# GATv2 on one Trainium2 core: order of the gathers, the table products and the logits in a three-layer edge loop

## The chip, the core and the metric

The kernel runs on one core of a Trainium2 chip. A core has five engines that work side by side, each through its own instructions in order: TensorE (PE in the profile, with its weight loads as PEld), VectorE (DVE), ScalarE (ACT), GpSimd (POOL) and SyncE (SP, which here only starts transfers). They meet through semaphores. The matmul's results go to PSUM, which is cut into eight banks of 128 x 512 float32. Transfers between the device's memory and SBUF are started by SP, ACT and POOL.

The metric is the time of one execution in microseconds. The kernel before takes 4618.6 us, the median of three runs (4614.17 to 4620.98).

## What is computed

The whole program is a four-layer network on 1250 nodes with 512 features; the change lies in its first stage, a GATv2 of three layers. Cut to what matters:

```python
src2 = concatenate([src, loop]); dst2 = concatenate([dst, loop])
ea2 = concatenate([edge_attr, mean_ea])
for k in range(3):
    xl = x @ Wl[k] + bl[k]
    xr = x @ Wr[k] + br[k]
    ef = ea2 @ We[k]
    m = leaky_relu(xl[src2] + xr[dst2] + ef, 0.2)
    logit = m @ att[k]
    alpha = segment_softmax(logit, dst2)
    out = segment_sum(xl[src2] * alpha[:, None], dst2) + b_out[k]
    h = out + x
    x = relu(layernorm(h) * gamma[k] + beta[k])
```

For every edge the row `xl` of its source is fetched, the row `xr` of its destination and the edge's own term are added, and a weighted sum over the features gives the logit. The softmax runs over the edges that end at one node; the weighted sum of the fetched rows is the node's new value.

## The kernel before

The edges are sorted by destination and cut into 12 blocks of 107 nodes. A layer has 188 tiles of 128 edges (`FT`), in 47 groups of four (`FG`, `GE = 4`); four groups make a block. `gat_layer` (L1198) runs one layer; its main loop (L1421 to L1445) takes one tile per step `i`, with `g, j = divmod(i, 4)`, and calls the small functions below; a framework turns their instructions into the engines' queues, with the waits that data and buffers ask for, and may move an instruction some places in its queue.

What one group goes through:

- `load(g)` (L1223): four gathers on POOL (L231), each fetching 128 rows `xl` of 513 numbers from the table `tl` (the 513th is the linear part of the logit), into one of nine buffers; at the head of a block the destinations' rows `hl` (SP, L1231 and L1232); the mask `nb` (SP, L1235, four buffers) and the edges' features, written straight into the one-hot tile `oh` (SP, L1237, three buffers). Called for groups 0 to 2 before the loop, then for g + 3 at j = 1.
- `onehot(g)` (L1243): ACT turns the mask into the one-hot matrix; for g + 1 at j = 2.
- `right(i)` (L1256, L1257): two matmuls on PE multiply the one-hot tile with the destinations' rows, high and low part, into an `mm` bank. For odd tiles under 16 (`on_pe`) a third (L1259) adds `xl`.
- `logits(i)` (L1269, L1272): VectorE adds `xl` to the bank (where PE has not), takes the negative part times `att` and sums it into `lg`. It runs one tile behind `right`.
- `spread(g)` (L1278, L1279, L1283, L1287): two VectorE adds of 128 x 4 bring the linear parts of node and edge into `lg`; PE transposes spread the logits; VectorE masks them and keeps the running minimum. At the end of a block ACT takes the exponentials (L1296), and `turn` (L1312, L1315) and `mix` (L1325, a bank of `more`) of the block's groups are put on the list `edge`, one mix a step. The last mix of a group frees its `xl` buffer.
- `finish(b)` (L1333): VectorE adds the residual `cur`; then a list `todo` of due steps: `norm`, `scale`, `relu` (with the multiplication by gamma and the addition of beta on POOL, L1368 and L1369, and the store), `across` (PE transposes L1378, ACT copies), and in layers 1 and 2 the products of the finished nodes with the next layer's weights, `gat_tables` (L1150): eight matmuls per 128 nodes (L1161; four into one `mm` bank for the left table, four for the right one), each pair of four followed by the eviction on ACT and VectorE (L1169, L1171; L1177, L1178) and a store by SP (L1173, L1179). The next layer's first gather waits for the last of these stores.
- `load_cur(b)` (L1408): SP loads the block's own rows `c`, and POOL adds `b_out` to them (L1413). `prepare` loads the next layer's weights and vectors, all at step 6.

The PSUM banks are `mm` 4, `tp` 2 (transposes), `more` 2. The products take turns with the edge tiles in the four `mm` banks. The list `todo` gives up one entry a step, two when it holds more than twelve. After the loop the rest of `edge` and `todo` is worked off, two of each at a time (L1446).

Of the kernel before, what the change touches and what calls it, by code (L numbers as in the profile page):

```python
# [37 lines left out]
GE = 4  # L38
# [19 lines left out]
class Net:  # L58
# [46 lines left out]
    @contextmanager  # L105
    def psum(self, mm=4, tp=4, more=0):

        with self.tc.tile_pool(name="psum", bufs=1, space=bass.MemoryType.PSUM) as self.ps:
            self.banks = {"mm": mm, "tp": tp, "more": more}
            yield  # L110

    @contextmanager
# [997 lines left out]
    def gat_weights(self, L, p):  # L1110


        nc, I, k = self.nc, self.I, L["k"]
        L["wl"] = self.weight(I["L0_gnn_Wl"][k], 4, D)
        L["wr"] = self.weight(I["L0_gnn_Wr"][k], 4, D)
        v = p.tile([128, D], F32, tag="v", name="we")
        nc.sync.dma_start(v[0:2], I["L0_gnn_We"][k])
        nc.sync.dma_start(v[2:3], I["L0_gnn_bl"][k].unsqueeze(0))
        more = p.tile([128, D], F32, tag="v", name="br")
        nc.gpsimd.memset(more[:16], 0.0)  # L1120
        for i in range(2):
            nc.sync.dma_start(L["tr"][NP:, i, :], more[:16])
        nc.sync.dma_start(L["ends"][:8, 1, :], more[:8])
        nc.sync.dma_start(more[2:3], I["L0_gnn_br"][k].unsqueeze(0))
        nc.gpsimd.tensor_tensor(v[:3], v[:3], more[:3], op=ALU.add)
        hl = p.tile([128, 2, D], F32R, tag="tro", name="wehl")
        nc.scalar.copy(hl[:3, 0], v[:3])
        nc.gpsimd.tensor_tensor(hl[:3, 1], v[:3], hl[:3, 0].bitcast(F32), op=ALU.subtract)
        for r in range(0, 8, 2):
# [17 lines left out]
        nc.vector.scalar_tensor_tensor(L["ae"], self.rec[:, :, 3], cs[1], L["ae"],  # L1147
                                       op0=ALU.mult, op1=ALU.add)

    def gat_tables(self, L, p, t, xT):  # L1150


        nc = self.nc
        ts = slice(t * 128, (t + 1) * 128)
        d = {}

        def product(name, c):
            def f():
                if c == 0:
                    d[name] = self.mm()  # L1160
                nc.tensor.matmul(d[name], lhsT=xT(c), rhs=L[name][:, c, :], start=c == 0,  # L1161
                                 stop=c == 3)
                if c == 3:
                    (left if name == "wl" else right)(d[name])
            return f

        def left(m):
            o = p.tile([128, D + 1], F32, tag="tlo", name="tlo")
            nc.scalar.copy(o[:, :D], m)  # L1169
            junk = p.tile([128, D], F32, tag="junk", name="junk", bufs=1)  # L1170
# [27 lines left out]
    def gat_layer(self, L, p, xtab, otab, big):  # L1198
# [4 lines left out]
        nxt = None if k == 2 else {}  # L1203

        def prepare():
            for name in ("b_out", "bl", "gamma", "beta"):
                vec[name] = p.tile([128, D], F32, tag=name, name=name, bufs=1)
                nc.sync.dma_start(vec[name], I["L0_gnn_" + name][k].unsqueeze(0)
                                  .to_broadcast([128, D]))
            nc.gpsimd.tensor_tensor(vec["b_out"], vec["b_out"], vec["bl"], op=ALU.add)  # L1210
            if nxt is not None:
                nxt.update(self.gat_vectors(k + 1, p))
                self.gat_weights(nxt, p)
                self.gat_linear(nxt, p, p)

        todo = deque()
        edge = deque()
        step = [0]

        def block(g):  # L1220
# [2 lines left out]
        def load(g):  # L1223
# [17 lines left out]
        def onehot(g):  # L1241
            d = G[g]
# [32 lines left out]
        def spread(g):  # L1275
            d = G[g]
            b, k, last = block(g)
            nc.vector.tensor_tensor(d["lg"], d["lg"], d["xl"][:, :, D], op=ALU.add)  # L1278
            nc.vector.tensor_tensor(d["lg"], d["lg"], L["ae"][:, g * GE:(g + 1) * GE],  # L1279
                                    op=ALU.add)  # L1280
# [52 lines left out]
        def finish(b):  # L1333
# [21 lines left out]
            def scale():  # L1355
# [7 lines left out]
                else:  # L1363
                    nc.vector.scalar_tensor_tensor(rs[:R, 1:2], mv[:R, 0:1], -1.0, rs[:R, 0:1],
                                                   op0=ALU.mult, op1=ALU.mult)
                    nc.scalar.activation(h[:R], h[:R], AF.Identity, scale=rs[:R, 0:1],
                                         bias=rs[:R, 1:2])
                    nc.gpsimd.tensor_tensor(h[:R], h[:R], vec["gamma"][:R], op=ALU.mult)  # L1368
                    nc.gpsimd.tensor_tensor(h[:R], h[:R], vec["beta"][:R], op=ALU.add)  # L1369

# [4 lines left out]
            def across():  # L1375
# [30 lines left out]
        cur = {}  # L1406

        def load_cur(b):  # L1408
            R = min(BN, NP - b * BN)
            c = p.tile([128, D], F32, tag="c", name="c")  # L1410
            for lo, hi in ((0, BW),) if b < NB - 1 else ((0, 96), (96, R)):
                nc.sync.dma_start(c[lo:hi], xtab[b * BN + lo:b * BN + hi, :])
            nc.gpsimd.tensor_tensor(c[:R], c[:R], vec["b_out"][:R], op=ALU.add)  # L1413
            cur[b] = c

        for g in range(3):
            load(g)
        onehot(0)  # L1420
        for i in range(FT + 2):  # L1421
            g, j = divmod(i, GE)
            step[0] = i
            if j == 1 and g + 3 < FG:
                load(g + 3)
            if j == 2 and g + 1 < FG:
                onehot(g + 1)
            if i == 6:
                prepare()
            if i % 16 == 8 and i < FT:  # L1430
                load_cur(i // 16)
            if i < FT:
                right(i)
            if 1 <= i <= FT:
                logits(i - 1)
            if j == 1 and 1 <= g <= FG:
                spread(g - 1)
            while edge and edge[0][0] <= i:
                _, f, product = edge.popleft()
                f()  # L1440
                if product:
                    break
            for _ in range(2 if len(todo) > 12 else 1):
                if todo and todo[0][0] <= i:
                    todo.popleft()[1]()  # L1445
        while edge or todo:  # L1446
            for _ in range(2):
                if edge:
                    edge.popleft()[1]()
            for _ in range(2):  # L1450
                if todo:
                    todo.popleft()[1]()
        return nxt

    def run(self, fast):
# [65 lines left out]
    def gat_first(self, pv, xtab):  # L1521
        nc, I = self.nc, self.I
        L = self.gat_vectors(0, pv)
        with self.tc.tile_pool(name="l0", bufs=1) as p, \
# [3 lines left out]
            with self.tc.tile_pool(name="edge", bufs=1, side="right") as pe, \  # L1528
                    self.weights(), self.psum(4, 3, 1):
                self.edge_pool = pe  # L1530
                self.gat_weights(L, pt)
                self.prepare_edges()
                for t in range(NT):
                    self.ready(t)
# [12 lines left out]
                def steps():  # L1547
                    for t in range(NT):
                        for i, f in enumerate(self.gat_tables(
                                L, pt, t, lambda c: xnT[:, c, t * 128:(t + 1) * 128])):  # L1550
                            f()
                            if i % 4 == 3:
                                yield
# [1570 lines left out]
```

## Time and profile before

| | us |
|---|---|
| median of three runs (lowest, highest) | 4618.6 (4614.17, 4620.98) |
| the profiled execution | 4626.03 |
| its span | 4624.2 |
| layer 1 of the stage, first gather to the next layer's first gather | 312.9 to 775.7 |
| layer 2 | 775.7 to 1235.9 |
| layer 3, to its end | 1235.9 to 1661 |
| PE, DVE, ACT, POOL busy over the span | 3950, 2760, 1507, 1361 |
| mean TensorE clock granted | 0.925 of full speed |

The span is the profiled execution from its first to its last instruction. A busy share over the whole span says little, since the program has a dozen stages with different limits; the stage of the change takes 29% of it. Windows (stretches of the span, with each engine's busy time in them) show one stage at a time, and the rows of an engine show what it was doing and, in brackets, how long it had been idle and which instruction released it. "issue" and "remote" there are waits for which the profile names no instruction. A wait is put down to whatever came last.

### The profile page before, as it was taken

What the parts mean: (1) busy time and instruction counts of PE and PEld (TensorE: products, weight loads), DVE (VectorE), ACT (ScalarE), POOL (GpSimd) and SP (SyncE); (2) the same over time, 40 slices, a digit from 0 to 9 for tenths busy, and PEclk for the clock granted to TensorE, in tenths of its full rate; (3) what the DMA queues carried; (4) which work ended last, traced back from release to release, by engine and by line L of the source; (5) the groups of instructions that cost most, each with busy time, mean ns of one, the idle gap of its engine ahead of it and who ended that gap; (6) DMA issues with size and microseconds to landing.
All of it is one profiled execution on the core that took longest, in us unless ns stands there. A gap on an engine that the chain in (4) does not pass through costs nothing.

```text
span 4624.2 us, 49180 instructions
## 1 busy us (share of the span) xinstructions
PE 3950.4 (85%) x15439; PEld 2438.3 (53%) x15454; DVE 2760.3 (60%) x6534; ACT 1506.7 (33%) x2738; POOL 1361.1 (29%) x1198
## 2 busy tenths in 40 slices
PE   6978997899878876799899999997969975898796
PEld 3435553455444443444788877564536553454574
DVE  5358884888488966533796767314693135587301
ACT  2213332343233355111374346222221022455121
POOL 2026663566356501101100000103253003676101
PEclk9998998899989977899999999998989997998798
DMA  6446664566456612411521110382011285565695
GB/s 221 149 124 193 183 190 140 165 185 190 128 168 180 172 63 77 139 33 35 161 65 41 56 34 28 138 318 95 12 54 62 73 271 164 156 202 175 234 339 191
DMA packets 282999, 647.56 MB, mean 140 GB/s; under 512 B 61673, under 2 KB 108905, under 8 KB 267322
## 3 DMA queue, kind: packets, MB, share of 16 engines
q1 hardware_dynamic: 169290, 357.13, 23.7%
q0 software_dynamic: 73088, 234.75, 18.0%
q10 hardware_dynamic: 40352, 52.44, 3.4%
q8 instruction: 126, 2.06, 0.2%
q14 instruction: 143, 1.17, 0.1%
HBM read 528.87 MB, written 120.65 MB: 140 GB/s over the span
## 4 chain that ended last, share of the span: by engine, by line
PE 32%; DVE 9%; DMA 5%; issue 3%; ACT 2%; POOL 1%; SPq 0%; another core or an unknown queue 0%; ACTq 0%; POOLq 0%; DVEq 0%
PE more L2051 5%; PE mm L2601 4%; PE mm L1914 3%; PE mm L179 3%; PE mm L171 3%; PE mm L3039 2%; DMA xe<-routed_in 2%; PE mm L776 2%; PE mm L2295 2%; PE mm L2013 1%; PE more L2877 1%; PE mm L2290 1%; DVE junk L1942 1%; DVE e L1976 1%; PE mm L2405 1%
## 5 line engine op out<-in xcount | busy, mean ns | idle before, releaser
L231 POOL DMA_INDIRECT xl<-xl,srcI x564 | 610.8, 1083 | 404.1 <-PE more L1325 167.6
L1325 PE MATMUL more<-xl,wT 128*128 128x512 f32 x1128 | 584.9, 611 | 5.5 <-ACT wT L1315 5.5
L1256 PE MATMUL mm<-hl,oh 121*128 121x512 f32 x564 | 399.1, 708 | 103.6 <-DVE s L1269 66.7
L1269 DVE TENSOR_TENSOR s<-xl,mm 128x512 f32<-128x512 f32 x540 | 364.0, 680 | 170.2 <-PE mm L1257 80.8
L1272 DVE SCALAR_TENSOR_TENSOR junk<-s,att 128x512 f32<-128x512 f32 x540 | 405.0, 750 | 5.5
L2051 PE MATMUL more<-hh,e 128*128 128x259 f32 x1600 | 384.2, 386 | 11.7 <-ACT o L1994 9.4
L2051 PEld LDWEIGHTS more<-hh,e 128*128 128x128 f32 x1600 | 295.0, 191 | 76.3 <-issue 16.0
L171 PE MATMUL mm<-w,xnT 128*128 128x512 f32 x640 | 307.0, 619 | 13.8 <-DVE xnT L136 5.3
L231 POOL DMA_INDIRECT g<-routed_out,getI x60 | 66.5, 1109 | 681.5 <-DMA routed_out<-o 494.7
L1325 PEld LDWEIGHTS more<-xl,wT 128*128 128x128 f32 x1128 | 207.0, 196 | 92.2 <-issue 44.2
L1257 PE MATMUL mm<-hl,oh 121*128 121x512 f32 x564 | 242.5, 430 | 0.0
L231 POOL DMA_INDIRECT hs<-gcn_h,srcI x188 | 213.5, 1136 | 95.6 <-issue 35.5
L1256 PEld LDWEIGHTS mm<-hl,oh 121*128 121x128 f32 x564 | 112.6, 200 | 226.9 <-issue 115.2
L1243 ACT ACTIVATE oh<-nb 112x512 fp32r<-112x512 bf16 x141 | 88.6, 629 | 356.1 <-DMA nb<-nbt 241.9
L171 PEld LDWEIGHTS mm<-w,xnT 128*128 128x128 f32 x640 | 123.4, 198 | 141.9 <-issue 125.2
L1971 ACT ACTIVATE e<-r,hh 128x512 f32<-128x512 f32 (+1 forms) x240 | 154.1, 646 | 131.8 <-PE more L2051 120.9
L2601 PE MATMUL mm<-form,cw 128*128 128x312 f32 (+1 forms) x640 | 175.5, 436 | 21.8 <-POOL cw L2578 18.2
L2877 PE MATMUL more<-hl,oh 128*128 128x512 f32 x376 | 162.0, 532 | 35.0 <-DVE hl L2838 9.8
L1974 ACT ACTIVATE e<-r,a 128x512 f32<-128x512 f32 (+1 forms) x240 | 152.3, 646 | 70.6 <-DVE e L1976 58.5
L1976 DVE TENSOR_TENSOR e<-e,e 128x512 f32<-128x512 f32 (+1 forms) x240 | 141.6, 596 | 50.9 <-ACT e L1971 44.6
L1315 ACT COPY wT<-tp 128x512 f32<-128x512 f32 x141 | 82.3, 584 | 267.4 <-PE tp L1312 212.8
L160 PE MATMUL tp<-ident,xn 128*128 128x128 f32 x280 | 51.4, 331 | 135.2 <-issue 56.2
(618 smaller groups left out, 7894.0 us busy)
## 6 DMA issues: line engine op xcount, KB each, us to landing
w<-L_ffn_Wp SPq DMA_DIRECT2D x64, 1024.0 KB
w<-L_ffn_table SPq DMA_DIRECT2D x56, 1025.0 KB
neg<-ntab SPq DMA_DIRECT2D x80, 320.0 KB
nb<-nbt SPq DMA_DIRECT2D x141, 128.0 KB
hl<-xr SPq DMA_DIRECT2D x36, 448.0 KB
xr<-tro SPq DMA_DIRECT2D x30, 512.0 KB
xe<-routed_in SPq DMA_DIRECT2D x56, 256.0 KB
routed_out<-o ACTq DMA_DIRECT2D x56, 256.0 KB
```

The source lines that it names most:

```text
L171: self.nc.tensor.matmul(p, lhsT=xT[:, c, t * 128:(t + 1) * 128], rhs=w[:, c, n0:n0 + n], start=c == 0, stop=c == k - 1)
L231: self.nc.gpsimd.indirect_dma_start(out=out, out_offset=None, in_=table, in_offset=bass.IndirectOffsetOnAxis(ap=idx, axis=0), bounds_check ...
L1256: nc.tensor.matmul(m, lhsT=s, rhs=hl[:K, 0, :], start=True, stop=False)
L1257: nc.tensor.matmul(m, lhsT=s, rhs=hl[:K, 1, :], start=False, stop=not on_pe(i))
L1269: nc.vector.tensor_tensor(o, d["xl"][:, j, :D], s, op=ALU.add)
L1272: nc.vector.scalar_tensor_tensor(junk, s, 0.0, L["att"], op0=ALU.max, op1=ALU.mult, accum_out=d["lg"][:, j:j + 1])
L1325: nc.tensor.matmul(B[b]["y"], lhsT=d["wT"][:, j, :], rhs=d["xl"][:, j, :D], start=k == 0 and j == 0, stop=last and j == GE - 1)
L1971: nc.scalar.activation(e1[:, :n], R[q, k, 0][:, :n], AF.Exp, bias=HH[q][:, s, 256:257])
L1976: nc.vector.tensor_tensor(e1[:, :n], e1[:, :n], e2[:, :n], op=ALU.max)
L2051: nc.tensor.matmul(ys[j], lhsT=e[:, j * 128:(j + 1) * 128], rhs=HH[q][:, s, :], start=s == 0, stop=s == NT - 1)
L2601: nc.tensor.matmul(m, lhsT=g[:, which, c, :], rhs=forms[form][:, c, q % 2, q // 2:q // 2 + n], start=j + c == 0, stop=j + 1 == len(gs) and ...
L2877: nc.tensor.matmul(y, lhsT=oh, rhs=hl[:, i], start=i + j == 0 and not (self.fast and k), stop=last and i + j == GE)
```

## The change

What it does, part by part:

- One PSUM bank, `tab`, is set apart for the table products; `mm` has three banks. `gat_tables` is given the function that hands out the bank. The products go to a list of their own, `late`, which gives up one every second step (every step while it holds more than eight); they are put there when `across` is issued. `todo` gives up one a step.
- `load` keeps the gathers and `hl`; the mask and the edge features move to `fields(g)`, called for g + 2 at j = 2 (0 and 1 before the loop).
- `linear(g)`, a POOL add of the two linear parts into `lin` (two buffers), stands at j = 1 ahead of the gathers of g + 3; VectorE's `spread` adds `lin` alone.
- `onehot(g + 1)` moves to j = 1; `logits` runs two tiles behind `right`, `spread` at j = 2; the loop has one step more. `on_pe` covers odd tiles under 20.
- POOL's add on `c` becomes `bias_cur`, twelve steps after the load; gamma and beta become `affine`, five steps after `finish`; `relu` follows at nine and `across` (or the last layer's `add`) at twelve.
- `prepare` and `gat_weights` become generators that go on every third step from step 6.

```diff
-            self.banks = {"mm": mm, "tp": tp, "more": more}
+            self.banks = {"mm": mm, "tp": tp, "more": more, "tab": 8 - mm - tp - more}
...
-    def gat_tables(self, L, p, t, xT):
+    def gat_tables(self, L, p, t, xT, bank):
...
-                    d[name] = self.mm()
+                    d[name] = bank()
...
+            G.setdefault(g, {})["xl"] = xl
+
+        def fields(g):
             nb = p.tile([128, GE * 128], BF16, tag="nb", name="nb", bufs=4)
             nc.sync.dma_start(nb, self.nbt[g])
             s = p.tile([128, GE * 128], F32R, tag="oh", name="oh", bufs=3)
             nc.sync.dma_start(s[BW:K].bitcast(F32),
                               self.eat[:, g * GE * 128:(g + 1) * GE * 128])
-            G[g] = {"xl": xl, "nb": nb, "s": s}
+            G.setdefault(g, {}).update(nb=nb, s=s)
+
+        def linear(g):
+            lin = p.tile([128, GE], F32, tag="lin", name="lin")
+            nc.gpsimd.tensor_tensor(lin, G[g]["xl"][:, :, D], L["ae"][:, g * GE:(g + 1) * GE],
+                                    op=ALU.add)
+            G[g]["lin"] = lin
...
-            return i < 16 and i % 2 == 1
+            return i < 20 and i % 2 == 1
...
-            nc.vector.tensor_tensor(d["lg"], d["lg"], d["xl"][:, :, D], op=ALU.add)
-            nc.vector.tensor_tensor(d["lg"], d["lg"], L["ae"][:, g * GE:(g + 1) * GE],
-                                    op=ALU.add)
+            nc.vector.tensor_tensor(d["lg"], d["lg"], d["lin"], op=ALU.add)
...
+                for t in whole:
+                    for f in self.gat_tables(nxt, p, t, lambda c, t=t: X[t][:, c, :],
+                                             lambda: self.bank("tab", [128, D])):
+                        late.append((step[0] + 1, f))
...
-            todo.extend(((now + 1, norm), (now + 3, scale), (now + 8, relu)))
+            todo.extend(((now + 1, norm), (now + 3, scale), (now + 5, affine),
+                         (now + 9, relu)))
             if nxt is None:
-                todo.extend((now + 11, add(t)) for t in whole)
+                todo.extend((now + 12, add(t)) for t in whole)
             else:
-                todo.append((now + 11, across))
-                for t in whole:
-                    for f in self.gat_tables(nxt, p, t, lambda c, t=t: X[t][:, c, :]):
-                        todo.append((now + 12, f))
+                todo.append((now + 12, across))
...
+        fields(0)
         for g in range(3):
             load(g)
+        fields(1)
         onehot(0)
-        for i in range(FT + 2):
+        prepared = prepare()
+        for i in range(FT + 3):
             g, j = divmod(i, GE)
             step[0] = i
-            if j == 1 and g + 3 < FG:
-                load(g + 3)
-            if j == 2 and g + 1 < FG:
-                onehot(g + 1)
-            if i == 6:
-                prepare()
+            if j == 1:
+                if g < FG:
+                    linear(g)
+                if g + 3 < FG:
+                    load(g + 3)
+                if g + 1 < FG:
+                    onehot(g + 1)
+            if j == 2 and g + 2 < FG:
+                fields(g + 2)
+            if i >= 6 and i % 3 == 0:
+                next(prepared, None)
             if i % 16 == 8 and i < FT:
                 load_cur(i // 16)
+            if i % 16 == 4 and i > 16:
+                bias_cur(i // 16 - 1)
             if i < FT:
                 right(i)
-            if 1 <= i <= FT:
-                logits(i - 1)
-            if j == 1 and 1 <= g <= FG:
+            if 2 <= i < FT + 2:
+                logits(i - 2)
+            if j == 2 and 1 <= g <= FG:
                 spread(g - 1)
...
-            for _ in range(2 if len(todo) > 12 else 1):
-                if todo and todo[0][0] <= i:
-                    todo.popleft()[1]()
-        while edge or todo:
+            if todo and todo[0][0] <= i:
+                todo.popleft()[1]()
+            if late and late[0][0] <= i and (i % 2 == 0 or len(late) > 8):
+                late.popleft()[1]()
+        bias_cur(NB - 1)
+        while edge or todo or late:
...
-        with self.psum(4, 2, 2):
+        with self.psum(3, 2, 2):
             self.gatv2_fast(L, xtab)
```

More of the change, by code (lines that the diff above doesn't have):

```diff
@@ L1124, in gat_weights @@
         nc.sync.dma_start(more[2:3], I["L0_gnn_br"][k].unsqueeze(0))
+        yield
         nc.gpsimd.tensor_tensor(v[:3], v[:3], more[:3], op=ALU.add)
+        yield
         hl = p.tile([128, 2, D], F32R, tag="tro", name="wehl")
         nc.scalar.copy(hl[:3, 0], v[:3])
+        yield
         nc.gpsimd.tensor_tensor(hl[:3, 1], v[:3], hl[:3, 0].bitcast(F32), op=ALU.subtract)
+        yield
         for r in range(0, 8, 2):
@@ L1209, in prepare @@
                                   .to_broadcast([128, D]))
-            nc.gpsimd.tensor_tensor(vec["b_out"], vec["b_out"], vec["bl"], op=ALU.add)
+            steps = iter(())
             if nxt is not None:
                 nxt.update(self.gat_vectors(k + 1, p))
-                self.gat_weights(nxt, p)
+                steps = self.gat_weights(nxt, p)
+                next(steps)
+            yield
+            nc.gpsimd.tensor_tensor(vec["b_out"], vec["b_out"], vec["bl"], op=ALU.add)
+            for _ in steps:
+                yield
+            if nxt is not None:
                 self.gat_linear(nxt, p, p)
@@ L1217, in gat_layer @@
         edge = deque()
+        late = deque()
         step = [0]
@@ L1367, in scale, with affine @@
                                          bias=rs[:R, 1:2])
+            def affine():
+                if not tail:
                     nc.gpsimd.tensor_tensor(h[:R], h[:R], vec["gamma"][:R], op=ALU.mult)
@@ L1412, in load_cur, with bias_cur @@
                 nc.sync.dma_start(c[lo:hi], xtab[b * BN + lo:b * BN + hi, :])
+            cur[b] = c
+        def bias_cur(b):
+            c = cur[b]
+            R = min(BN, NP - b * BN)
             nc.gpsimd.tensor_tensor(c[:R], c[:R], vec["b_out"][:R], op=ALU.add)
-            cur[b] = c
+        fields(0)
         for g in range(3):
             load(g)
+        fields(1)
         onehot(0)
-        for i in range(FT + 2):
+        prepared = prepare()
+        for i in range(FT + 3):
             g, j = divmod(i, GE)
             step[0] = i
-            if j == 1 and g + 3 < FG:
-                load(g + 3)
-            if j == 2 and g + 1 < FG:
-                onehot(g + 1)
-            if i == 6:
-                prepare()
+            if j == 1:
[9 more added lines that the diff above has]
+                next(prepared, None)
             if i % 16 == 8 and i < FT:
                 load_cur(i // 16)
+            if i % 16 == 4 and i > 16:
+                bias_cur(i // 16 - 1)
             if i < FT:
                 right(i)
-            if 1 <= i <= FT:
-                logits(i - 1)
-            if j == 1 and 1 <= g <= FG:
+            if 2 <= i < FT + 2:
+                logits(i - 2)
+            if j == 2 and 1 <= g <= FG:
                 spread(g - 1)
@@ L1452, in gat_layer @@
                     todo.popleft()[1]()
+            for _ in range(2):
+                if late:
+                    late.popleft()[1]()
         return nxt
@@ L1530, in gat_first @@
                 self.edge_pool = pe
-                self.gat_weights(L, pt)
+                for _ in self.gat_weights(L, pt):
+                    pass
                 self.prepare_edges()
@@ L1549, in steps @@
                         for i, f in enumerate(self.gat_tables(
-                                L, pt, t, lambda c: xnT[:, c, t * 128:(t + 1) * 128])):
+                                L, pt, t, lambda c: xnT[:, c, t * 128:(t + 1) * 128],
+                                self.mm)):
                             f()
```

## The prediction

> **What bounds the kernel now.** I read the whole page first, then the windows of the stage that the change touches, then the row of VectorE (DVE) and GpSimd (POOL) at the head of a layer, then the waits. The page's chain of waits reaches back only to 2215 us, so it says nothing here; the stage (three GATv2 layers) lies from 312.9 us, layer 1's first gather, to 1661 us, and what it loses is read from its own windows. Columns: window and length, then busy time (count) of PE, PEld, DVE, ACT, POOL, then clock, DMA share and GB/s.
>
> ```profile
> 776.00:830.00 54.00, 25.67 (x54) 13.40 (x55) 16.76 (x47) 1.05 (x2) 36.24 (x36) 0.56 0.69 195
> 830.00:1180.00 350.00, 324.53 (x1154) 185.66 (x1153) 303.02 (x794) 137.34 (x252) 204.38 (x181) 0.97 0.62 177
> 1186.00:1236.00 50.00, 45.43 (x129) 21.32 (x127) 13.29 (x33) 14.37 (x28) 3.04 (x3) 0.97 0.25 79
> 1236.00:1286.00 50.00, 21.65 (x49) 10.30 (x48) 13.00 (x35) 1.26 (x2) 35.92 (x36) 0.70 0.72 204
> 1286.00:1630.00 344.00, 291.99 (x1029) 169.77 (x1030) 314.55 (x832) 125.95 (x230) 204.76 (x182) 0.94 0.59 168
> ```
>
> Three kinds of time. A ramp (776 to 830, 1236 to 1286): POOL issues 36 gathers, nine buffers of four, and PE and DVE are idle more than half of it. A steady part: in layer 2 PE 93% and DVE 87% busy, in layer 3 (no table products) DVE 91%. A tail (1186 to 1236): PE alone, 45 of 50 us.
>
> Inside layer 2's ramp, DVE's and POOL's rows (start, us, [idle before and releaser]):
>
> ```profile
> 796.38 0.69 DVE L1269 TENSOR_TENSOR s<-xl,mm 128x512 f32<-128x512 f32 x1 [4.79 <-remote]
> ...
> 809.03 0.69 DVE L1269 TENSOR_TENSOR s<-xl,mm 128x512 f32<-128x512 f32 x1 [11.36 <-issue]
> ...
> 823.76 0.69 DVE L1269 TENSOR_TENSOR s<-xl,mm 128x512 f32<-128x512 f32 x1 [12.62 <-remote]
> ```
>
> ```profile
> 777.03 1.01 POOL L231 DMA_INDIRECT xl<-xl,srcI  x1 [0.30 <-issue]
> 778.35 1.00 POOL L231 DMA_INDIRECT xl<-xl,srcI  x1 [0.30 <-issue]
> ```
>
> The gathers come every 1.30 us from 775.7 to 822.9. Their rows landed in time; yet DVE waits 11 and 13 us for matmuls whose rows on PE had ended (the L1257 of 813.78 is over at 814.4, DVE starts at 823.76). No releaser is named. What is visible is the coincidence: DVE is starved while POOL issues without a pause, and runs at full rate from 824 us, when POOL stops; layer 3 does the same (gaps of 6 and 13 us, full rate from 1287; POOL stops at 1282.9). Counting DVE's L1272 starts sixteen tiles at a time gives the block times (a block is 16 tiles): first block 39.3, 50.1 and 49.9 us in the three layers, later ones 27.8 to 31 us without products, 33.5 to 37 with products, layer 3 about 32.4.
>
> **The change, part by part.** All sums are against the profiled execution: 4626.0 us (span 4624.2 and 1.8 around it), 7.4 above the median of 4618.6.
>
> *Fewer gathers ahead.* The new add `lin` of a group stands in POOL's queue ahead of the gathers three groups on, has two buffers, and so waits for VectorE's add of two groups earlier. In the changed program's order POOL issues groups 0 to 4 freely, group 5 after spread(0), group 6 after spread(1). spread(0)'s adds ran 11 to 13 us after the first gather, spread(1)'s at 30 (layer 3) and 35 us (layer 2). So POOL now pauses after 24 to 28 gathers, 31 to 36 us in, not after 36 (47 us): 8 to 12 gathers x 1.30 = 10.4 to 15.6 us sooner. In that time DVE did two or three tiles anyway (2 us each), leaving 6 to 10; I take 9 for layers 2 and 3, and 3 for layer 1, whose first block lost only half as much: -21. Bounds: nothing, if POOL's issuing isn't the cause; all that first blocks lose against 28 us, 11 + 22 + 22 = -55. Later gathers are no danger: the group is fetched about four groups (32 us) before use and four gathers take 5.2 us.
>
> *Products every second step, own bank, three `mm` banks.* A step costs PE about 1.33 us (two right-hand matmuls and a mix; spacing of the rows), a product 0.86 more; in before eight come in consecutive steps, which makes these PE-bound at 2.2 to 2.6 us while DVE waits 0.7 to 1.5 us a step ("DVE s L1269 <- PE mm L1257", 33.5 us in layer 1's steady part), and the other steps are DVE-bound. PE's floor for such a block is 16 x 1.33 + 8 x 0.86 + 8 x 0.45 (transposes) + 0.45 = 32.2 us against 34.9 measured, 2.5 us x 13.5 blocks = -34 at best. I take two fifths, because DVE's own floor (31 us with its two 0.68 us evictions) is close: -14. Fewer banks cost nothing in the loop: products sat in one of the four, so the tiles had three before; VectorE, two tiles behind, still finds two results ready. If they were short, every step would pay the handshake, up to 1 us x 188.
>
> *One add less on VectorE.* The pair and what POOL's own big adds cost, for the stage:
>
> ```profile
> L1278 DVE TENSOR_TENSOR lg<-lg,xl 128x4 f32<-128x4 f32 x141 | 55.7, 395 | 0.6
> L1279 DVE TENSOR_TENSOR lg<-lg,ae 128x4 f32<-128x4 f32 x141 | 32.1, 228 | 0.5
> L1413 POOL TENSOR_TENSOR c<-c,b_out 107x512 f32<-107x512 f32 x33 | 43.9, 1332 | 82.1 <-DMA c<-x 78.3 <-issue 3.2
> L1907 POOL MEMSET hh<- 128x10 f32 x8 | 0.8, 120 | 287.7 <-PE more L2051 218.6 <-DVE r L1988 69.1
> ```
>
> Half of 87.8 goes: 44 us, of which DVE's bound parts (layer 3, blocks without products) give 0.4: -18. Low: only the median of 0.158 x 141 = 22 at 0.4, -9. High: the whole dearer one at 91%, -51. Two more PE-added tiles a layer trade 0.68 us of DVE for 0.86 of PE and cancel. The new POOL add isn't in the trace: between L1907's 0.12 us and L1413's 1.33 us; four elements a partition are nearest to the former, so about 0.2 us x 141, hidden under POOL's idle 40% (204 of 350 us busy).
> L1278's typical time is 0.158 us, but 28 of 141 took up to 1.71 us, beside a POOL add. The Trainium skill (GPSIMD Engine Reference, 8. Key points, and 4.1 Engine selection) says that POOL shares its SBUF interfaces with VectorE, contending with VectorE instructions of two SBUF inputs, and that an elementwise add belongs on VectorE, being about twice as slow on POOL. It speaks against this part: 141 more POOL adds would each hold a VectorE add. By the rule, with nothing saved, this term would be 0 in place of -18 and the forecast about 4594; by the row the hold lasts as long as the POOL add, so a short one holds little.
>
> *Moves.* Affine, bias and `prepare` only leave POOL waiting less (the 78.3 us for c in the row above); POOL wasn't the bound, so zero. Uncovered, that wait is what delays gathers. Behind each `lin` stand gathers, affine and bias_cur, and the next spread waits for it; it is emitted five steps (10 us) before VectorE needs it. Behind SP's nb/eat loads, now three steps before the one-hot, stand the table stores; ACT waited for nb before too, 241.9 us, at no cost.
>
> *Tail.* In the changed order 27 products and 22 mixes follow the last right-hand product of a layer, 24 and 21 before: 4 x 0.86 = 3.4 us of PE where PE is the bound. With one bank a product pair of four must be evicted (0.68 to 1.5 us) before the next begins, partly under mixes: about 1.6. Two layers: +10; high end, seven evictions of 1.5 bare, +28.
>
> Sum: -21 - 14 - 18 + 10 = -43: 4583 for the profiled execution, 4576 for the median.
>
> **Rivals.**
> *Ramps stay.* The stall has another cause (no releaser is named, which speaks for it; its end with POOL's last gather in two layers speaks against): -14 - 18 + 10 = -22, 4597.
> *All of it.* Ramp -45, products -28, adds -35, tail +5 = -103: 4516. For it: PE at 0.56 and 0.70 clock in the ramps, so the idle feeds itself. Against: DVE's floor of 31 us in product blocks.
> *Slower: POOL in one chain.* `lin`, gathers, affine and bias now release VectorE in order. If `lin` costs over 1 us, POOL's block is 16 x 1.30 + 4 x 1.3 + 3 x 1.33 = 30 us, plus 1.8 for ACT at affine (54.5 us over 30 at L1368) and about 2 for buffers: 34, against 30 to 32 in some 17 product-free blocks: +60 at 3.5 each; with the ramp and the tail +49, product and add gains lost: 4668. For it: POOL's in-order waits already reach 24.8 us on "PE more L1325". Against: a 128x10 POOL memset of 0.12 us and five steps of slack. It decides from about 1 us a `lin`.
> *It doesn't limit.* spread(0) and (1) could come so early that POOL never pauses; then a ramp is short for the same reason. No case of its own.
>
> **How the numbers follow.** Forecast 0.48 (own range 4530 to 4608), ramps stay 0.18, all of it 0.13, POOL chain 0.21. Under 0.2% (9 us) a measurement of this kernel can't tell. Faster: 0.48 + 0.13 + most of 0.18 = 0.72; same 0.06; slower 0.22. The range 4515 to 4640 leaves out half of "all of it" and most of the chain: about 0.2.
>
> **What would show it.** Right: POOL's first pause after 24 to 28 gathers, DVE's gaps in the ramp ending with it, first blocks near 41 us in layers 2 and 3; product blocks near 33.5 us with products two steps apart; one 128x4 add a group; tails 3 to 6 us longer. Wrong: VectorE waiting for `lin`, POOL over 80% busy, gaps that outlast POOL's pause, or steady blocks over 36 us.

## The result and the profile after

The changed kernel takes 4591.0 us, the median of nine runs (4578.4 to 4602.8), against 4620.2 us before (4614.1 to 4628.6): a ratio of 0.9921, with a 95% interval of 0.9904 to 0.9937. The profiled execution of after takes 4585.9 us, 40 less than that of before; its stage of three layers runs from 312.7 to 1627.6 us, about 33 us shorter. The other 7 us lie in code that the change doesn't touch, and are no part of it. The medians differ by 29 us: the profiled execution of before lies 6 us above its median and that of after 5 us below, so 11 of the 40 us are the luck of this pair.

The windows of after that answer to those of before (length, then busy time and count of PE, PEld, DVE, ACT, POOL, clock, DMA share, GB/s): the first 54 us of layer 2, its tail, and the first 50 us of layer 3.

```profile
770.90:824.90 54.00, 33.45 (x79) 18.00 (x80) 24.62 (x66) 6.06 (x12) 39.98 (x43) 0.65 0.71 214
1162.40:1214.90 52.50, 47.38 (x131) 21.77 (x130) 12.71 (x31) 14.44 (x29) 2.65 (x2) 0.97 0.24 83
1214.90:1264.90 50.00, 24.99 (x59) 13.42 (x60) 19.46 (x50) 2.33 (x4) 33.81 (x37) 0.74 0.67 198
```

In the ramps VectorE does half as much again in the same time (24.6 us of work against 16.8, and 19.5 against 13.0). The tail is 3 us longer and PE has 2 us more to do in it.

The rows at the head of layer 2, first VectorE's waits of 3 us or more for nothing that is named (start, us, [idle before and releaser]), then GpSimd's first wait for VectorE:

```profile
786.99 0.16 DVE L1302 TENSOR_TENSOR lg<-lg,lin 128x4 f32<-128x4 f32 x1 [3.67 <-issue]
...
807.29 0.69 DVE L1293 TENSOR_TENSOR s<-xl,mm 128x512 f32<-128x512 f32 x1 [6.46 <-remote]
```

```profile
814.23 1.00 POOL L231 DMA_INDIRECT xl<-xl,srcI  x1 [0.30 <-issue]
818.98 0.19 POOL L1261 TENSOR_TENSOR lin<-xl,ae 128x4 f32<-128x4 f32 x1 [3.75 <-DVE lg L1302]
819.74 1.43 POOL L231 DMA_INDIRECT xl<-xl,srcI  x1 [0.57 <-issue]
```

GpSimd now stops after 32 gathers, and the instruction that it stops at is the new add, waiting for VectorE's add of two groups earlier: the fetch limit at work. Before, it stopped after 36 for want of a buffer. VectorE's longest gaps, which had been 11.4 and 12.6 us, are 3.7 and 6.5. The longer one ends at 807.29, 8 us before GpSimd stops. In layer 3, the last long gap and the stop:

```profile
1260.51 0.69 DVE L1293 TENSOR_TENSOR s<-xl,mm 128x512 f32<-128x512 f32 x1 [9.81 <-remote]
```

```profile
1256.52 1.00 POOL L231 DMA_INDIRECT xl<-xl,srcI  x1 [0.30 <-issue]
1268.31 0.19 POOL L1261 TENSOR_TENSOR lin<-xl,ae 128x4 f32<-128x4 f32 x1 [10.78 <-DVE lg L1302]
```

Here too GpSimd stops after 32 gathers, and VectorE's gap ends 3 us later.

The three layers cut in the same way in both profiles, in us. The ramp ends at the start of the seventeenth tile (L1272, now L1296), the tail begins at the start of the last one:

| | before: ramp, steady, tail | after: ramp, steady, tail | difference |
|---|---|---|---|
| layer 1 | 52.1, 357.3, 53.4 | 50.6, 350.9, 56.7 | -1.5, -6.4, +3.3 |
| layer 2 | 57.4, 353.3, 49.5 | 47.2, 344.3, 52.5 | -10.2, -9.0, +3.0 |
| layer 3 | 57.9, 336.1, 31.1 | 52.5, 329.3, 30.8 | -5.4, -6.8, -0.3 |

So -17 in the ramps, -22 in the steady parts, +6 in the tails. A second pair of profiles (before2 and after2 below) has -12 (+4.4, -10.0 and -6.5 by layer), -22 and about +5: layer 1's ramp says nothing, and the rest comes again.

### The profile page after: what moved, and what is told of

Same layout as the page of the kernel before. It is cut to its first block, busy times and chain, and to the rows that moved or that the text cites. A ratio compares the mean times of both kernels' runs of the same rounds, so it can differ in the third digit from the quotient of the medians.

```text
span 4584.0 us, 49281 instructions
## 1 busy us (share of the span) xinstructions
PE 3946.8 (86%) x15451; PEld 2434.6 (53%) x15466; DVE 2706.4 (59%) x6387; ACT 1502.9 (33%) x2738; POOL 1402.3 (31%) x1339
## 3 DMA queue, kind: packets, MB, share of 16 engines
q1 hardware_dynamic: 169290, 357.13, 23.5%
## 5 line engine op out<-in xcount | busy, mean ns | idle before, releaser
L1280 PE MATMUL mm<-hl,oh 121*128 121x512 f32 x564 | 419.6, 744 | 89.7 <-DVE s L1293 29.7
L1296 DVE SCALAR_TENSOR_TENSOR junk<-s,att 128x512 f32<-128x512 f32 x534 | 409.8, 767 | 6.2
L1347 PEld LDWEIGHTS more<-xl,wT 128*128 128x128 f32 x1128 | 196.5, 192 | 86.2 <-ACT wT L1337 34.4
L1281 PE MATMUL mm<-hl,oh 121*128 121x512 f32 x564 | 238.2, 422 | 0.0
L1280 PEld LDWEIGHTS mm<-hl,oh 121*128 121x128 f32 x564 | 111.6, 198 | 232.6 <-issue 135.0
L1166 PE MATMUL tab<-w,xT 128*128 128x512 f32 x320 | 165.1, 614 | 19.9 <-DVE junk L1176 18.1
L1281 PEld LDWEIGHTS mm<-hl,oh 121*128 121x128 f32 x564 | 113.1, 201 | 106.9 <-issue 105.4
```

What stands on the lines that cost most here:

```text
L1280: nc.tensor.matmul(m, lhsT=s, rhs=hl[:K, 0, :], start=True, stop=False)
L1281: nc.tensor.matmul(m, lhsT=s, rhs=hl[:K, 1, :], start=False, stop=not on_pe(i))
L1296: nc.vector.scalar_tensor_tensor(junk, s, 0.0, L["att"], op0=ALU.max, op1=ALU.mult, accum_out=d["lg"][:, j:j + 1])
L1347: nc.tensor.matmul(B[b]["y"], lhsT=d["wT"][:, j, :], rhs=d["xl"][:, j, :D], start=k == 0 and j == 0, stop=last and j == GE - 1)
```

## The experiments

Twelve runs were made, in four groups; the kernels of one group ran on one chip, with the kernel before beside them. It turned out that the chips differ: on one kind the kernel before takes about 4620 us (the first pair of profiles and the second group), on the other about 4552 (the other three groups).

**Four edits alone.** The limit taken away by more buffers for `lin`, the limit drawn tighter, the add and limit undone, the bank undone.

```diff
 e1_lin12, e2_lin1
-            lin = p.tile([128, GE], F32, tag="lin", name="lin")
+            lin = p.tile([128, GE], F32, tag="lin", name="lin", bufs=12)   # e2_lin1: bufs=1
 e3_dveadds (also e3_again, e3_third)
-                if g < FG:
-                    linear(g)
-            nc.vector.tensor_tensor(d["lg"], d["lg"], d["lin"], op=ALU.add)
+            nc.vector.tensor_tensor(d["lg"], d["lg"], d["xl"][:, :, D], op=ALU.add)
+            nc.vector.tensor_tensor(d["lg"], d["lg"], L["ae"][:, g * GE:(g + 1) * GE], op=ALU.add)
 e4_shared
-                                             lambda: self.bank("tab", [128, D])):
+                                             self.mm):
-        with self.psum(3, 2, 2):
+        with self.psum(4, 2, 2):
```

> The changed kernel with twelve buffers for lin in place of two, so that the add no longer holds the gathers back and POOL may fill all nine xl buffers at once again. Theory (the fetch limit is what shortened the ramps): the first blocks of layers 2 and 3 grow back from 40.8 and 47.9 us to 50 to 54, the steady blocks stay, total about 4591 + 15 = 4606 (ratio to before 0.995 to 0.998). Rival (the ramps shortened through the other order on SP and the moved prepare): first blocks stay at 41 and 48 us, total 4591 (ratio 0.992).

> The changed kernel with one buffer for lin, so that gathers run one group less ahead. Theory: POOL's first pause comes after 20 to 24 gathers, not 28 to 32, first blocks 5 us shorter in layers 2 and 3 (36 and 43 us), steady blocks the same, total 4591 - 10 = 4581 (ratio 0.990). Rival (POOL's order becomes a chain with VectorE): steady blocks grow by a wait of VectorE for lin, over 1 us a block, total above 4591, up to 4625. Second rival (the depth doesn't matter): 4591 with unchanged ramps.

> The changed kernel without lin: both 128x4 adds on VectorE as before, and no fetch limit. Theory: ramps as in the run with twelve lin buffers (first blocks 50 to 54 us), and the second add back, 44 us of VectorE at a share of 0.4, so about 10 to 18 us above that run: 4616 to 4624 (ratio 0.999 to 1.001). Rival (the add was hidden, PE bounds the steady part): equal to the run with twelve buffers within 4 us.

> The changed kernel with the products back in four shared mm banks, still one every second step. Theory (product blocks are bound by PE's 32.7 busy us, the bank is not their limit): product blocks 34.5 to 35.5 us as now, the tails 1 to 3 us shorter each because a product pair needn't wait for the eviction, total 4591 - 4 = 4587 (ratio 0.991). Rival (the bank of its own is a part of the gain): product blocks 1 us or more longer, total 4600 to 4610.

Measured, beside a kernel before of 4552.5 us: twelve buffers 4778.4 (ratio 1.049, 1.047 to 1.051); one buffer 4552.2 (1.0001, 0.9984 to 1.0017); adds on VectorE 4540.9 (0.9981, 0.9968 to 0.9993); shared banks 4558.6 (1.0007, 0.9994 to 1.002). None of the expectations on ramps could be judged: the first blocks of layers 2 and 3 took 26 to 30 us in all four kernels, 36 gathers in a row or not. On this chip there was no stall to shorten.

The run with twelve buffers missed for another reason. Its `lin` on GpSimd up to 1700 us, 132 of the stage's 141 (count, busy us and mean ns, then idle time before and what ended it):

```profile
L1261 POOL TENSOR_TENSOR lin<-xl,ae 128x4 f32<-128x4 f32 x132 | 36.4, 277 | 345.8 <-DMA xl<-xl,srcI 332.4 <-issue 12.9
```

and the same group in the changed kernel:

```profile
L1261 POOL TENSOR_TENSOR lin<-xl,ae 128x4 f32<-128x4 f32 x141 | 47.5, 337 | 81.9 <-DVE lg L1302 78.9 <-issue 0.4
```

With buffers to spare the framework moves each `lin` forward, right behind the gathers of its own group, and GpSimd then stands still until these have landed: 332 us of waiting, with the next gathers and gamma and beta queued behind it. Product blocks of 35 us become 39 to 46 (one 56), and layer 3's later blocks grow from 32 us to 35 or more. So the two buffers do two things: they bound the depth, and they keep the add away from its own gather. This edit therefore didn't test the depth alone.

One buffer (1.0001) against two (0.9994 on another chip of this kind, below) makes no difference that can be told; how it does where the ramps stall wasn't run. The bank of its own makes none either: a product block of the run with shared banks, and one of the changed kernel,

```profile
961.00:996.70 35.70, 32.74 (x119) 18.61 (x118) 27.43 (x75) 13.86 (x26) 22.02 (x23) 1.00 0.66 182
```

```profile
967.90:1003.50 35.60, 32.73 (x118) 18.46 (x117) 27.53 (x73) 13.62 (x26) 22.27 (x23) 1.00 0.66 185
```

are the same within 0.1 us, with PE busy 32.7 us in both. The tails of layers 1 and 2, which were to shrink with shared banks, take 56.4 and 54.7 us; with a bank of its own 55.6 and 52.3 on the third group's chip.

**Is it the chip?** The kernel before and the changed one, unchanged, with profiles, and the products at every step:

```diff
 e5_everystep
-            if late and late[0][0] <= i and (i % 2 == 0 or len(late) > 8):
+            if late and late[0][0] <= i and True:
```

> The kernel before, unchanged, with a profile on the chip of this call. In the last call the first blocks of layers 2 and 3 took 26 to 30 us in all kernels, where the first pair of profiles had 40.8 to 53.4 us. Theory (the stall of the ramps belongs to the chip that the first pair ran on): first blocks 26 to 31 us here too, total about 4552. Rival (the kernels of the last call removed it): 50 to 54 us.

> The changed kernel, unchanged. If the chip doesn't stall: layers 2 and 3 gain nothing in the ramp, steady blocks as in the first profile (product blocks 35.3 us, the last layer's 32), tails 3 us longer, ratio to before 0.998 to 1.002. If the ramp's gain doesn't depend on the chip: ratio 0.992 as in the first pair.

> The changed kernel with a product at every step instead of every second one, in its one bank. Theory (product blocks are bound by PE's 32.7 busy us, so the spacing adds nothing): product blocks 34.5 to 36 us, total within 5 us of the changed kernel. Rival (the spacing balances PE and VectorE, the prediction's -14): product blocks 1 us longer or more, total 10 to 15 us above the changed kernel.

This group ran on a chip of the first kind. Before: one profiled run of 4629.3 us, median of the runs beside it 4621.7, first blocks of layers 2 and 3 at 52.4 and 53.0 us: the rival of that expectation. The changed kernel 4588.6 us (0.9932, 0.9908 to 0.9956), first blocks 40.6 and 46.7: the first result again. Products at every step: 4592.8 (0.994, 0.9916 to 0.9963). From the first gather to the seventeenth tile, by the gathers that GpSimd had issued before it first let 5 us or more pass from one gather's start to the next:

| gathers before the pause | kernels | us to the seventeenth tile |
|---|---|---|
| 36 (layers 2 and 3) | before, before2 | 57.4, 56.7, 57.9, 57.5 |
| 32 in layer 3 | after, after2, e5_everystep | 52.5, 51.0, 49.6 |
| 32 in layer 2 | after, after2, e5_everystep | 47.2, 46.7, 46.7 |

(In layer 2 the small add and an add of `prepare` stand between two gathers after 28, whose starts are 2.6 us apart; the wait for VectorE comes after 32.) With the same 32 gathers, layer 2 gains 10 to 11 us and layer 3 5 to 8.

With a product at every step the product blocks are shorter, not longer. Two of them, and the last block but one of the same layer:

```profile
965.00:998.00 33.00, 32.46 (x117) 18.38 (x116) 29.02 (x73) 13.28 (x25) 21.83 (x24) 1.00 0.67 199
1032.40:1066.80 34.40, 32.60 (x117) 18.37 (x116) 29.10 (x74) 13.53 (x25) 22.21 (x24) 1.00 0.65 198
1094.90:1132.50 37.60, 34.18 (x117) 19.32 (x116) 29.21 (x73) 13.44 (x26) 22.52 (x25) 0.95 0.65 185
```

The layer's five blocks full of products (the fifth to the ninth) take 169.0 us, 33.0 to 34.4 each, where the spacing of two takes 174.4 and 175.3 in its two profiles; what is won there goes in the last three blocks (+4 in this layer, +9 in layer 1). Theory and rival both missed the sign; the total is the same.

**The pair on one chip, and the stall's cause.** The kernel without `lin`, the changed one, and one in which SP fetches plain rows, so that GpSimd starts no gather:

```diff
 e6_spplain
-                self.gather(xl[:, j, :], L["tl"][:, :], self.srcI[:, t:t + 1])
+                nc.sync.dma_start(xl[:, j, :], L["tl"][9 * 128:10 * 128, :])
```

> The changed kernel without lin (both adds on VectorE, no fetch limit), beside the changed kernel on one chip; it was 0.998 of the kernel before on a chip whose ramps don't stall. On a chip that stalls (kernel before near 4620 us): theory (the fetch limit makes the ramp's gain): first blocks of layers 2 and 3 at 50 to 54 us, against 41 and 47 for the changed kernel, total 4600 to 4610 in spite of steadier blocks. Rival (the ramp's gain comes from the other parts): first blocks at 41 to 48 us and a total at or under the changed kernel's. On a chip that doesn't stall: 8 to 12 us under the changed kernel, layer 3's blocks at 30 to 31 us against 32, because POOL's affine no longer waits behind lin.

> The changed kernel as the partner of the run without lin. Chip that stalls: 0.992 to 0.994 of the kernel before. Chip that doesn't: 0.999 to 1.001, as the run with one lin buffer.

> The changed kernel with every gather replaced by a plain load of 128 rows of the table's last tile, started by SP; the same bytes arrive, but POOL starts no transfer. The output isn't the reference's: the source rows are wrong. Theory (the ramp stalls while POOL issues): no gaps of 6 us or more in VectorE's row of the first blocks, first blocks under 33 us on any chip. Rival (the traffic of the fetched rows stalls PE): gaps as before on a chip that stalls, first blocks 40 to 54 us.

The chip was of the second kind (kernel before 4553.6 us). There the change is worth nothing: 4550.3 us, 0.9994 (0.9978 to 1.0011). The first 54 us of layer 2 and the first 50 of layer 3 of the changed kernel on it:

```profile
772.70:826.70 54.00, 39.79 (x129) 22.88 (x129) 36.34 (x100) 10.17 (x19) 43.35 (x48) 0.84 0.80 234
1209.50:1259.50 50.00, 35.42 (x114) 19.05 (x113) 32.89 (x90) 9.54 (x18) 39.98 (x45) 0.90 0.76 219
```

The same instructions, and VectorE does 36.3 us of work in the window where on the first chip it did 24.6. GpSimd issues no slower (43.4 us busy), the DMA engines move more (234 GB/s). So continuous issue alone doesn't stall VectorE; the stall comes with it on the first kind of chip only.

The run with plain loads, a single execution of 4492.8 us, couldn't tell what in the gathers stalls, for want of a stall. Its first blocks of layers 2 and 3 take 20.8 and 22.3 us (26.5 and 28.3 in the changed kernel beside it), that of layer 1 37.0, over the 33 expected. It showed something else. A steady block of layer 3 in it, and one of the changed kernel on the same chip:

```profile
1387.10:1415.80 28.70, 25.29 (x98) 15.14 (x97) 28.48 (x75) 11.70 (x23) 5.74 (x7) 1.00 0.65 210
```

```profile
1364.10:1396.40 32.30, 26.20 (x97) 14.89 (x96) 28.87 (x76) 12.00 (x23) 22.75 (x24) 1.00 0.66 189
```

VectorE has nearly the same work, 28.5 and 28.9 us. Without gathers it is the bound (99% busy); with them it waits 3.4 us a block, though GpSimd is busy only 70%. (Layer 3's fifth to eleventh blocks take 28.2 to 31.8 us without gathers, 31.4 to 32.9 with them.)

**No lin, once more, and the last layer's add later.**

```diff
 e8_lateadd
                 def f():
-                    o = p.tile([128, D], F32, tag="h", name="o")
-                    nc.sync.dma_start(o, otab[t * 128:(t + 1) * 128, :])
-                    self.add_to_x(t, o)
-                    self.ready(t)
+                    cur["o", t] = p.tile([128, D], F32, tag="o", name="o")
+                    nc.sync.dma_start(cur["o", t], otab[t * 128:(t + 1) * 128, :])
+                def last():
+                    self.add_to_x(t, cur.pop(("o", t)))
+                    self.ready(t)
-                return f
+                return f, last
...
-                todo.extend((now + 12, add(t)) for t in whole)
+                adds = [add(t) for t in whole]
+                todo.extend((now + 12, f) for f, _ in adds)
+                todo.extend((now + 22, f) for _, f in adds)
```

> The changed kernel without lin (both adds on VectorE, no fetch limit) once more, to have it on a chip whose ramps stall if this call's chip is one (kernel before near 4620 us). There: theory (the fetch limit makes the ramp's gain): first blocks of layers 2 and 3 at 50 to 54 us, POOL's first long pause after 36 gathers, total 4600 to 4615. Rival (the other order of the first instructions makes it): 40 to 48 us, total 4575 to 4590. On a chip that doesn't stall: 0.998 to 1.000 of the kernel before, as in the two earlier runs.

> The changed kernel with the last layer's add into x split from its load: the load at twelve steps after finish as now, VectorE's add and the row statistics at twenty-two. Theory (layer 3's blocks of 32 us are held by VectorE waiting 2.5 us a block for that load, 26 us in all): layer 3's blocks 30 us, 10 to 20 us under the changed kernel: ratio to before 0.988 to 0.991 on a chip that stalls, 0.996 on one that doesn't. Rival (the wait was cover for PE's and GpSimd's chain): the same as the changed kernel, 0.993 and 0.9994.

Again a chip of the second kind (before 4551.0). Without `lin`: 4539.5 us, 0.9978 (0.9962 to 0.9994); in the third group, beside the changed kernel, it had been 4548.7, 0.9996 (0.9982 to 1.0011), 1.6 us under the changed kernel and not the 8 to 12 expected. With the later add: 4546.7, 0.9991 (0.9978 to 1.0005), the rival's side. VectorE's waits in the last layer, later add first, then the changed kernel of the third group, then the kernel without `lin` (waits in us, times, longest):

```profile
DVE x L185 <- DMA o<-x: 35.4, 9, 6.4
```

```profile
DVE x L185 <- DMA o<-x: 28.1, 9, 5.7
```

```profile
DVE x L185 <- DMA o<-x: 18.7, 7, 5.7
```

Putting the add later didn't take VectorE's wait away. Leaving out `lin` took a third of it. The chain behind it is seen on ScalarE, whose relu waits for GpSimd's gamma and beta: in the stage, the same changed kernel and kernel without `lin`,

```profile
ACT h L1397 <- POOL h L1394: 120.7, 30, 8.1
```

```profile
ACT h L1399 <- POOL h L1396: 80.3, 29, 7.5
```

against 87.2 us before (on the first kind of chip). `lin` waits for VectorE, gamma and beta wait behind `lin`, ScalarE's relu and store behind them, and the reload of `o` and VectorE's add into x behind the store. This chain is read from the waits; no run took one link alone. In single profiles on this kind of chip layer 3, from its first gather to the start of its last tile, takes 367 to 372 us with `lin` in one or two buffers, 360 with `lin` and the later add, and 356 to 362 without `lin`.

## Why the prediction was right, point by point

The total came out inside the range, and two of the four terms (ramps and tails) near their sizes. The other two did not do what they were counted for, and a gain that no term names stands in their place; that part of the agreement is luck.

*Ramps, -21 forecast, -17 measured (-12 in the second pair).* The size was near, the way to it only in part. The step that was mis-sized is the pause, "after 24 to 28 gathers, 31 to 36 us in": it came after 32, because VectorE's adds of the second group, for which the forecast had GpSimd wait, now ran 24 us after the first gather, before GpSimd came to them. GpSimd stopped 44 us (layer 2) and 43 us (layer 3) after the first gather where it had stopped after 47, so the limit can have won 3 and 4 us, not 10 to 16. In layer 3 that is most of the gain (5.4, and 6.5 in the second pair). In layer 2 (10.2 and 10.0) most was won before the limit acted: when GpSimd stopped, VectorE had begun 14 tiles, where before it had begun 10 and 12, three microseconds later. What shortened the stall there stays open, and that the limit won the rest wasn't isolated: the kernel without it never met a chip that stalls. Counting the starts of all tiles, the first blocks of before were 41.1, 53.0 and 53.4 us, 2 to 3.5 more than the prediction read; those of after are 39.1, 40.8 and 47.9.

What the forecast didn't know is that the stall belongs to some chips only. On the other kind its rival "ramps stay" is the right account of this term, for the opposite reason: they have no stall.

*Products, -14 forecast, none measured in the blocks full of products.* The five of them took 174.1 and 174.8 us in layers 1 and 2 before, 175.7 and 174.4 after. The step that failed is "two fifths of 2.5 us a block" (34.9 less 32.2 is 2.7): the floor of 32.2 us was near (PE is busy 32.5 to 32.7 us), but the distance to it wasn't made of the burst of products. The run with a product at every step, a burst again, came nearer to the floor than the spacing did (33.0 to 34.4 us). In the product block of before that starts at 993.2 us PE waits 2.1 us, for VectorE's `lg`; in that of after at 967.9 us it waits 1.5 us for `wT` and 1.1 us for the single bank:

```profile
PE tp L1283 <- DVE lg L1279: 2.1, 1, 2.1
```

```profile
PE more L1347 <- ACT wT L1337: 1.5, 1, 1.5
PE tab L1166 <- DVE junk L1176: 1.1, 1, 1.1
```

One wait went and two came. VectorE's waits of 0.7 to 1.5 us a step, which the step was built on, cost nothing that the spacing won back. VectorE's waits for ScalarE's copy of a product (L1171, now L1176) even grew from 42.5 to 97.4 us in the stage.

*The add, -18 forecast; 0 to -3 measured where it was to show, and the cause given not borne out.* VectorE's work fell by more than was counted: 87.8 us for two adds became 24.1 for one, and VectorE's busy time over the span fell by 54 us.

```profile
L1302 DVE TENSOR_TENSOR lg<-lg,lin 128x4 f32<-128x4 f32 x141 | 24.1, 171 | 6.1 <-issue 3.7 <-POOL lin L1261 1.8
L1296 DVE SCALAR_TENSOR_TENSOR junk<-s,att 128x512 f32<-128x512 f32 x534 | 409.8, 767 | 6.2
```

But the time didn't follow. Layer 3's fourth to eleventh blocks, where VectorE was taken for the bound, before and after:

```profile
1350.10:1608.80 258.70, 218.60 (x771) 127.11 (x770) 236.10 (x622) 98.11 (x177) 169.12 (x151) 0.95 0.65 186
1321.20:1577.30 256.10, 214.27 (x774) 122.56 (x772) 229.37 (x588) 95.26 (x176) 180.63 (x184) 0.98 0.64 187
```

VectorE has 6.7 us less to do, and the eight blocks are 2.6 us shorter; in the second pair 259.8 and 259.7 us. Nearly all of the -22 of the steady parts lies elsewhere, in both pairs alike: -10 in the three layers' second blocks (30.2, 27.8 and 27.8 us before, 27.0, 25.2 and 23.5 after), right behind the ramp, and -11 and -10 in the fourth and eleventh blocks of layers 1 and 2, from which products moved away (20 product matmuls a layer before, 14 or 15 after; at half of 0.86 us each, about 5 us of it). What shortens the second blocks (more tiles added on PE, logits two behind, or less to catch up after a shorter stall) stays open: no run separated these on a chip that stalls, and where nothing stalls the whole change is worth nothing.

There, too, the kernel that keeps both adds on VectorE is no slower: 0.9978 to 0.9996 where the changed kernel was at 0.9994. So the add's work was not on the path, and "VectorE is 91% busy in layer 3, hence the bound" was the wrong reading: on that kind of chip its blocks had 3 us of waiting, in part behind GpSimd's chain, which the new add lengthens.

The rule that was weighed against this part is in the Trainium skill (GPSIMD Engine Reference, 8. Key points, and 4.1 Engine selection). Of the contention that it names the trace shows this: the 128 x 4 adds, 395 and 228 ns before, are one of 171 ns now, and the two-input L1296 rose from 750 to 767 ns, 10 us in 564. Its long cases (44 over 0.9 us) all lie beside a GpSimd add of 512 numbers; a `lin` alone held nothing so long. So the 141 new adds took little back. That an add is about twice as slow on GpSimd does not show at this size: a `lin` typically takes 0.21 us, VectorE's add 0.16.

*Tails, +10 forecast, +6 measured (about +5 in the second pair).* PE has 2 us more to do in layer 2's, as counted; the single bank cost less than was allowed, since shared banks made the tails no shorter.

*The rivals.* "POOL in one chain" didn't happen with two buffers, but its mechanism was there in small, and with twelve buffers it came in full, +5%, at a `lin` of 0.28 us: it decides not by the add's price, as the rival had it, but by what the add waits for.

## What to carry to other kernels

A busy share of 90% does not make an engine the bound: VectorE's 3 us of gaps a block were waits for others, and work taken off it bought next to nothing. A small instruction put into a busy queue costs what it waits for, not what it does, and a buffer count can decide where it stands. A gain measured on one chip should be measured on another before it is explained.

## What the runs showed of the hardware

The same kernel took 4612 to 4630 us where the ramps stalled (the first pair and one other group) and 4537 to 4568 on the chips of the three other groups. In this stage the difference lies in the ramps: the changed kernel takes 46.7 to 52.5 us from the first gather of layers 2 and 3 to the seventeenth tile on the slower kind, and 32.6 and 32.8 on the other, with gathers issued 1.30 us apart on both.

The trace's semaphore records, which lie behind the views, say more of the waits with no named releaser. In five profiles of the slower kind, VectorE has 26 waits of 3 us or more in these ramps for one semaphore alone, PE's. In 24 of them an update of it is on record within 0.06 us of VectorE's start: at 823.74 for the start at 823.76, 9.4 us after PE's rows end the last matmul. In the long waits shown in these pages that distance is 2 to 10 us. So what VectorE waits for there is PE's result or its signal, and not the gathered rows, of which the prediction says that they landed in time (these profiles give no landing times for them). PE's ends are modelled, so the trace doesn't tell whether the matmul or the signal is late.

These profiles also lack records. That of before holds 1408 of the 1787 updates that PE's instructions make from 313 to 1600 us, and 7960 of the 14624 that the landings of GpSimd's transfers make; eight profiles of the other kind lack at most six of either. Whether the missing records and the stall have one cause, and what differs between the chips, was not found.
